# Layer 0's weight preparation: butterflies of the gate and up weights on GpSimd, the down weights' scales applied earlier

## The chip, the cores and the metric

The kernel runs on one core of one Trainium2 chip. The metric is the time of one execution on the device in microseconds (us), and the median over several runs counts. A core has five engines that run their own instruction streams in order: TensorE (PE), which multiplies matrices and writes to PSUM; VectorE (DVE); ScalarE (ACT); GpSimd (POOL); and SyncE (SP), which here only issues DMAs. They wait for each other by semaphores. SBUF is the on-chip memory with 128 partitions, PSUM the accumulation memory.

## The reference: what is computed

The input x has 4 sequences of 512 tokens with 512 features. There are two layers, and each computes

```
xn = layernorm(x)
x  = x + attention(xn) * silu(ffn(xn))
```

Layer 0's attention is a softmax attention with 32 heads of 16 features and 8 key/value heads. Its feed-forward block works in a rotated basis, where `fwht` is the normalised Walsh-Hadamard transform over the last axis:

```
x      = fwht(x * SU_ug) / 64
up     = x @ W_up.T   * (Wscale_ug[:2048] * 64)
gate   = x @ W_gate.T * (Wscale_ug[2048:] * 64)
h      = silu(gate) * up                # 2048 wide
h      = fwht(h * SU_dp) / 64
out    = h @ W_down.T * (Wscale_dp * 64)
```

Layer 1 is a recurrent linear attention with a feed-forward block of signs of weights. The change doesn't touch it.

## The kernel before

The kernel never transforms the tokens. It transforms the weights of layer 0 once, so that the tokens meet plain matrix products. For the gate and up weights a transform of length 512 = 4 x 128 runs over the rows: the 4 blocks are mixed by two butterfly stages (sums and differences of blocks), and the 128 rows within a block by a product with a 128x128 Hadamard matrix that carries the signs `SU_ug` (`hs`). For the down weights it is 2048 = 16 x 128: a product with a matrix `h16`, a trip through memory (`wdt`) that rearranges the rows, and a product with `hmat`; the signs and scales `cdn` (one per row) and `drow` (`Wscale_dp`, one per column) are applied at the last eviction.

The work around the change, with its names:

- `load_raw(n)` (line 166) loads columns of the gate weights (n even) or the up weights (n odd) into a tile `raw` of 128 x 4 x 256 f32. There are n = 0 to 15 such tiles and three buffers.
- `mix(n, stage)` (line 240) calls `butterfly` (line 48) for a stage. Stage 0 reads `raw` and writes `tmp` (one buffer), stage 1 reads `tmp` and writes `raw` back. Each stage is a sum (line 52) and a difference (line 53), each with 128x512 f32 elements on DVE.
- `fold(n, j)` (line 247) multiplies half of `raw` by `hs` on PE (line 253). ACT copies the product as the high part of the weights into `fo` (line 256), DVE subtracts it to get the low part (line 257). After j = 1 the next `load_raw(n + 3)` is issued, and `fo` is stored to memory as `wS` for later sequences.
- `mix_down(q)` (line 268): the first product for the down weights (line 270), a copy out of PSUM by ACT (line 271), a store to `wdt`; after the last q four loads bring it back as `wdn`.
- `fold_down(a)` (line 279): the second product (line 281) into the PSUM tile `y`, of which there is one buffer, and its eviction by DVE with `cdn` and `drow` (line 282).

All this runs while the attention of the first sequence is on its way. The loop over u (line 532) hands out the work by units: per unit one `maxima` (two score products, line 418, and a DVE reduction of 128x1024 from PSUM, line 419, with one buffer of scores), one `exps` eleven units later (line 439 on PE, an exponential on ACT, line 441), one column block of the feed-forward block (from unit 16 on: `gate_up`, line 316, whose PE products are line 326, ACT's tanh line 332, DVE's line 333, ACT's copy line 336 and GpSimd's product `hT` line 337), and from a table `early` the butterflies, folds and first down transforms: `mix(n, 0)` three units and `mix(n, 1)` two units before the two halves of `fold(n)`, at units 12 + 2n and 13 + 2n. `fold_down` has units 32 to 47. Each eight units `values` (line 443) multiplies the exponentials by the values; the sums of the softmax go through memory in four DMA steps (`sum_d`, `rc`, `rec_d`, `sm`), and GpSimd multiplies by their reciprocals (line 465).

The order on an engine is not the order of the program text. A planner orders each engine's instructions by their place in the text and by its own estimate of when their inputs are ready; `inorder` (`keep_in_program_order`) pins single ones. Once planned, each engine takes its instructions strictly in order.

Of the kernel before, what the change touches and what calls it, by code (L numbers as in the profile page):

```python
# [12 lines left out]
AF = mybir.ActivationFunctionType  # L13
ALU = mybir.AluOpType
# [4 lines left out]
P = 128  # L19
NB, SEQ, DM = 4, 512, 512  # L20
NT = NB * SEQ // P
TB = SEQ // P
KC = DM // P
# [10 lines left out]
def kernel(ctx: ExitStack, tc: tile.TileContext, i: dict, out: bass.AP):  # L34
    nc = tc.nc

    def new(pool, shape, dtype, tag, **kw):
        return pool.tile(shape, dtype, tag=tag, name=tag, **kw)
# [6 lines left out]

        return ap.unsqueeze(1).to_broadcast([ap.shape[0], n, ap.shape[1]])

    def butterfly(eng, dst, src, dim, h, pin=lambda ins: ins):

        s = src.rearrange("p (n two h) f -> p n two h f", two=2, h=h)  # L50
        d = dst.rearrange("p (n two h) f -> p n two h f", two=2, h=h)
        pin(eng.tensor_tensor(d[:, :, 0], s[:, :, 0], s[:, :, 1], ALU.add))
        pin(eng.tensor_tensor(d[:, :, 1], s[:, :, 0], s[:, :, 1], ALU.subtract))

    def ln_params(pool, rows, tag):

# [44 lines left out]
    if True:  # L101
# [10 lines left out]
        wdn = new(awp, [P, NI, DM], F32, "wdn")  # L112
# [4 lines left out]
        cdn = new(awp, [P, NI], F32, "cdn")  # L117
        drow = new(awp, [P, DM], F32, "drow")
# [45 lines left out]
        raws, fos = {}, {}  # L164
# [15 lines left out]
        nc.sync.dma_start(su_ug, i["su_ug"])  # L180
        nc.sync.dma_start(wsc, i["wsc"])
        nc.sync.dma_start(su_dp, i["su_dp"])

        stage = [new(hp, [P, DM], F32, "hT", bufs=16) for _ in range(NI)]
        for q in range(NI):
# [23 lines left out]
        for h in (8, 16, 32, 64, 1, 2, 4):  # L209
            nxt = new(a0 if h == 64 else awp, [P, P], F32, "h16" if h == 64 else "hmat", bufs=1 if h == 64 else 2)  # L210
            butterfly(nc.vector, nxt.unsqueeze(2), hmat.unsqueeze(2), P, h, inorder)
            hmat = nxt
            if h == 64:
                h16 = nxt
# [23 lines left out]
        tmps = {}  # L238

        def mix(n, stage):  # L240
            if stage == 0:
                tmps[n] = new(a0, [P, KC, CQ], F32, "tmp")
                butterfly(nc.vector, tmps[n], raws[n], KC, 1)
            else:
                butterfly(nc.vector, raws[n], tmps[n], KC, 2)

        def fold(n, j):
            q, m = n // 2, n % 2
# [19 lines left out]
        def mix_down(q):  # L268
            ph = new(bmm, [P, DM], F32, "mm")
            nc.tensor.matmul(ph, h16, stage[q], start=True, stop=True)  # L270
            nc.scalar.copy(stage[q], ph)
            nc.sync.dma_start(wdt.rearrange("(p q) n -> q p n", q=NI)[q], stage[q])
            if q == NI - 1:
                for o in range(4):
                    nc.sync.dma_start(
                        wdn[:, ts(o, 4), :], wdt[ts(o, DM), :].rearrange("(a p) n -> p a n", p=P)
                    )

        def fold_down(a):
            ph = misc()  # L280
            nc.tensor.matmul(ph, hmat, wdn[:, a, :], start=True, stop=True)
            nc.vector.scalar_tensor_tensor(wdn[:, a, :], ph, cdn[:, a : a + 1], drow, ALU.mult, ALU.mult)

        vps, kTs, oTs, hTs, g0s, wcs, ths = {}, {}, {}, {}, {}, {}, {}

# [71 lines left out]
        def misc(dtype=F32):  # L357

            return new(bpy, [P, SEQ], dtype, "y") if piece[0] % 64 < 32 else new(bmm, [P, SEQ], dtype, "mm")
# [16 lines left out]
        def queries(b, v, jj):  # L376

            pq = misc()
            for k in range(KC):
                nc.tensor.matmul(  # L380
                    pq, wq[:, k, ds(256 * v + P * jj, P)], xnTs[b][:, k, :], start=(k == 0), stop=(k == KC - 1)
                )
            qd = qds[b, v, jj] = new(b0, [P, SEQ], F16, f"qd{jj}", bufs=1)
            nc.scalar.activation(qd, pq, AF.Copy, scale=0.25)
# [122 lines left out]
        keys_values(0)  # L507
        for jj in range(2):
            queries(0, 0, jj)
        nc.sync.dma_start(drow, i["wsc_dp"].to_broadcast([P, DM]))  # L510
        nc.sync.dma_start(wo, i["wo0"].rearrange("(k p) n -> p k n", p=P))

        ph = new(bmm, [P, KC, P], F32, "mm")
# [10 lines left out]
        for n in range(FF // P):  # L524
            u = LATE + 2 * n - 4
            for d, f in ((-3, lambda n=n: mix(n, 0)), (-2, lambda n=n: mix(n, 1)),
                         (0, lambda n=n: fold(n, 0)), (1, lambda n=n: fold(n, 1))):
                early.setdefault(u + d, []).append(f)
        for q in range(NI):
            early.setdefault(q, []).append(lambda q=q: mix_down(q))  # L530

        for u in range(NU + LAG + 1):
# [22 lines left out]
            if 16 <= v < 16 + NI:  # L555
                fold_down(v - 16)
# [297 lines left out]
    total, done, n = sum(x[0] for x in steps), 0.0, 0  # L854
# [17 lines left out]
    drow = new(cm, [P, DM], F32, "drow")  # L872
# [35 lines left out]
    raws = {}  # L908
# [19 lines left out]
    pin, yvs = [False], {}  # L928
# [472 lines left out]
    n = 0  # L1401
# [56 lines left out]
```

## Time and profile before

| What | Value |
|---|---|
| Median of 3 runs | 1495.93 us (1493.04 to 1501.23) |
| Profiled execution, span from first to last instruction | 1492.3 us (no other time is recorded for this execution) |
| PE busy | 1429.4 us (96%), 8144 instructions |
| DVE busy | 1035.8 us (69%) |
| ACT busy | 709.6 us (48%) |
| POOL busy | 313.5 us (21%), 304 instructions |
| Mean granted TensorE clock | 0.992 |
| Line 52 and 53, all butterflies of raw and tmp | 64 instructions, 0.68 us median each, from 15.4 to 152.2 us |
| Line 419, maxima | 256 x 1.22 us |
| Line 257, low part | 32 x 0.68 us |
| Line 282, eviction of the second down transform | 16 x 0.74 us, from 117.7 to 182.8 us |
| Line 271, eviction of the first down transform | 16 x 0.585 us, from 20.2 to 42.1 us |
| Line 337, POOL product hT | 64 x 1.32 us |

A line of the profile's stage view gives a stretch in us from the start of the span, its length, and then for PE, PE's weight loads (PEld), DVE, ACT and POOL the busy time with the number of instructions, then the granted clock, the DMA engines' busy share and GB/s. A line of the timeline gives start, duration, engine, line of the kernel, operation, output<-inputs with shapes, and in brackets the idle time before it with what ended it. Matmuls are pipelined, so that the next begins before the last one's recorded end.

### The profile page before, as it was taken

The numbers are of one execution on the slowest core, as the hardware profiler recorded it, in microseconds if no ns is written. First come the engines' busy times: TensorE is split into PE (matmuls) and PEld (weight loads), VectorE is DVE, ScalarE is ACT, GpSimd is POOL, SyncE is SP. The second block draws the span as 40 slices with busy tenths as digits, with TensorE's granted clock in tenths as the row PEclk, the third lists the DMA queues.
The fourth block names the chain that finished last, engine by engine and source line by source line (L and its number), as shares of the span: only waits on it lengthen the run. The fifth ranks groups of instructions, "written<-read, shape, count | busy, mean of one in ns | idle before, by whom it ended". The sixth has DMA issues, their size and how long they took to land. (4 is left out here: it accounts for less than half of the span.)

```text
span 1492.3 us, 22700 instructions
## 1 busy us (share of the span) xinstructions
PE 1429.4 (96%) x8144; PEld 855.6 (57%) x8144; DVE 1035.8 (69%) x1863; ACT 709.6 (48%) x1046; POOL 313.5 (21%) x304
## 2 busy tenths in 40 slices
PE   7999999999999999999999899999999999999998
PEld 3565533555335553356434576787568766776675
DVE  7999755765557655666525869768975799477746
ACT  4655554666446664466552434434353344323433
POOL 1112100322003220033100330045112531052001
PEclk9999999999999999999999999999999999999989
DMA  8865410475105741166103553434453354425532
GB/s 307 322 220 194 149 29 16 149 237 190 27 21 190 231 149 28 36 212 225 56 20 103 160 146 101 116 92 147 134 151 103 91 161 135 126 73 150 162 83 96
DMA packets 201793, 199.11 MB, mean 133 GB/s; under 512 B 65520, under 2 KB 153040, under 8 KB 200784
## 3 DMA queue, kind: packets, MB, share of 16 engines
q1 hardware_dynamic: 198624, 196.29, 41.9%
q10 hardware_dynamic: 3056, 1.37, 0.4%
q8 instruction: 64, 1.05, 0.3%
q14 instruction: 49, 0.40, 0.1%
HBM read 146.80 MB, written 46.19 MB: 129 GB/s over the span
## 5 line engine op out<-in xcount | busy, mean ns | idle before, releaser
L419 DVE TENSOR_REDUCE nmx<-sc 128x2 f32<-128x1024 f32 x256 | 312.3, 1220 | 159.1 <-PE st L439 147.3
L441 ACT ACTIVATE pe<-st 128x1024 f16<-128x1024 f32 x256 | 262.6, 1026 | 143.4 <-PE st L439 141.6
L344 PE MATMUL y<-wdn,hT 128*128 128x512 f32 x512 | 253.3, 617 | 3.0 <-DVE g L348 1.7
L326 PE MATMUL mm<-xr,wc 128*128 128x512 f32 x768 | 206.8, 410 | 0.0
L326 PEld LDWEIGHTS mm<-xr,wc 128*128 128x128 f32 x768 | 137.4, 189 | 48.4 <-issue 21.8
L337 POOL TENSOR_TENSOR hT<-hT,th 128x512 f32<-128x512 f32 x64 | 84.2, 1316 | 319.2 <-ACT hT L336 309.0
L344 PEld LDWEIGHTS y<-wdn,hT 128*128 128x128 f32 x512 | 87.0, 189 | 96.0 <-issue 88.5
L711 PE MATMUL pu<-xn1T,wp 128*128 128x512 f32 x288 | 129.9, 594 | 0.0
L941 PE MATMUL ph<-xsh,sg 128*128 128x512 f32 x256 | 113.0, 441 | 5.6 <-ACT sg L926 5.3
L418 PE MATMUL sc<-kT,qT 32*128 32x512 f16 x512 | 102.5, 385 | 7.8 <-DVE nmx L419 7.4
L926 ACT ACTIVATE sg<-sw 128x512 fp32r<-128x512 f32 x128 | 79.5, 625 | 55.2 <-PE y L972 32.2
L941 PE MATMUL ph<-xsl,sg 128*128 128x512 f32 x256 | 104.1, 407 | 0.7 <-DVE xsl L901 0.7
L418 PEld LDWEIGHTS <-qT 32*128 32x128 f16 x512 | 26.2, 91 | 131.8 <-issue 127.9
L465 POOL TENSOR_TENSOR oT<-os,sm 128x512 f16<-128x512 f32 x32 | 41.5, 1298 | 285.9 <-DMA sm<-rec_d 248.8
L439 PE MATMUL st<-qm,kT 32*128 32x512 f16 x512 | 100.0, 384 | 0.3 <-ACT pe L441 0.3
L946 ACT ACTIVATE hT<-ph,upsc 128x512 f32<-128x512 f32 x64 | 43.8, 685 | 94.3 <-PE ph L941 94.1
L711 PEld LDWEIGHTS pu<-xn1T,wp 128*128 128x128 f32 x288 | 54.0, 191 | 56.6 <-issue 54.8
L972 PE MATMUL y<-sg,hsh 128*128 128x512 f32 x256 | 83.0, 432 | 0.7 <-ACT sg L926 0.7
L1019 POOL TENSOR_TENSOR gm<-g,le 128x384 fp32r<-128x384 f32 x64 | 57.8, 921 | 83.0 <-PE pu L1020 52.0
L326 PE MATMUL mm<-xr,fo 128*128 128x512 f32 x256 | 73.2, 420 | 0.9 <-DVE fo L257 0.9
L972 PE MATMUL y<-sg,hsl 128*128 128x512 f32 x256 | 73.5, 400 | 0.0
L332 ACT ACTIVATE th<-mm,hwg 128x512 f32<-128x512 f32 x64 | 44.0, 688 | 56.0 <-PE mm L326 56.0
(302 smaller groups left out, 2370.2 us busy)
## 6 DMA issues: line engine op xcount, KB each, us to landing
wc<-wS SPq DMA_DIRECT2D x96, 512.0 KB
wS<-fo SPq DMA_DIRECT2D x16, 1024.0 KB
sw<-in_upT SPq DMA_DIRECT2D x64, 256.0 KB
sw<-in_downT SPq DMA_DIRECT2D x64, 256.0 KB
sm<-rec_d SPq DMA_DIRECT2D x128, 64.0 KB
raw<-in_w_gateT SPq DMA_DIRECT2D x8, 512.0 KB
hT<-in_w_downT SPq DMA_DIRECT2D x16, 256.0 KB
raw<-in_w_upT SPq DMA_DIRECT2D x8, 512.0 KB
```

The source lines that it names most:

```text
L326: nc.tensor.matmul(pgs[m], wcs[b, c, m][:, h, k, :], xrs[b][:, k, :], start=(k + h == 0), stop=(k == KC - 1 and h == 1))
L337: nc.gpsimd.tensor_tensor(hT, hT, ths[b, c], ALU.mult)
L344: nc.tensor.matmul(ys[t], hTs[b, c][:, ts(t, P)], wdn[:, c, :], start=(c == 0), stop=(c == NI - 1))
L418: nc.tensor.matmul(sc[:, j, :], qTs[n][rows, ts(t, P)], kTs[b, g // 4][rows, :], start=True, stop=True)
L419: nc.vector.tensor_reduce(nmxs[n][:, t, 2 * pr : 2 * pr + 2], sc, AX.X, ALU.max, negate=True)
L439: nc.tensor.matmul(st[:, j, :], kTs[b, g // 4][rows, ts(k, P)], qms[n][rows, :], start=True, stop=True)
L441: nc.scalar.activation(pes[u], st, AF.Exp)
L711: nc.tensor.matmul(pp, wps[b, n][:, k, 0:P], xn1Ts[b][:, k, :], start=(k == 0), stop=(k == KC - 1))
L926: tc.keep_in_program_order(nc.scalar.activation(sgs[b, c, m], raws[b, c, m], AF.Sign))
L941: ins = nc.tensor.matmul(ph, sgs[b, c, 0][:, ts(k, P)], xss[b][n][:, k, :], start=(k + n == 0), stop=(k == KC - 1 and n == 1))
L972: ins = nc.tensor.matmul(yss[b][t], hss[b, c][n][:, ts(t, P)], sgs[b, c, 1], start=(c + n == 0), stop=(c == NI - 1 and n == 1))
L1019: nc.gpsimd.tensor_tensor(gm, bc_in(s["g2"][:, t, u, x], P), bc_mid(le, 3), ALU.mult)
```

## The change

`butterfly` may put its differences on another engine than its sums. The butterflies of `raw` go to GpSimd, except the difference of the second stage for n = 3 to 15, which stays on VectorE: one operation in four. The row `drow` is loaded ahead of the weights instead of after the first queries; VectorE multiplies the first down transform by it while it leaves PSUM, in place of ScalarE's copy; and ScalarE instead of VectorE takes the second transform out of PSUM, with the scale `cdn` alone.

```diff
-    def butterfly(eng, dst, src, dim, h, pin=lambda ins: ins):
+    def butterfly(sums, dst, src, dim, h, pin=lambda ins: ins, differences=None):
...
-        pin(eng.tensor_tensor(d[:, :, 0], s[:, :, 0], s[:, :, 1], ALU.add))
-        pin(eng.tensor_tensor(d[:, :, 1], s[:, :, 0], s[:, :, 1], ALU.subtract))
+        pin(sums.tensor_tensor(d[:, :, 0], s[:, :, 0], s[:, :, 1], ALU.add))
+        pin((differences or sums).tensor_tensor(d[:, :, 1], s[:, :, 0], s[:, :, 1], ALU.subtract))
...
         nc.sync.dma_start(su_dp, i["su_dp"])
+        nc.sync.dma_start(drow, i["wsc_dp"].to_broadcast([P, DM]))
...
                 tmps[n] = new(a0, [P, KC, CQ], F32, "tmp")
-                butterfly(nc.vector, tmps[n], raws[n], KC, 1)
+                butterfly(nc.gpsimd, tmps[n], raws[n], KC, 1)
             else:
-                butterfly(nc.vector, raws[n], tmps[n], KC, 2)
+                butterfly(nc.gpsimd, raws[n], tmps[n], KC, 2, differences=nc.vector if n > 2 else nc.gpsimd)
...
             nc.tensor.matmul(ph, h16, stage[q], start=True, stop=True)
-            nc.scalar.copy(stage[q], ph)
+            nc.vector.tensor_tensor(stage[q], ph, drow, ALU.mult)
...
             nc.tensor.matmul(ph, hmat, wdn[:, a, :], start=True, stop=True)
-            nc.vector.scalar_tensor_tensor(wdn[:, a, :], ph, cdn[:, a : a + 1], drow, ALU.mult, ALU.mult)
+            nc.scalar.activation(wdn[:, a, :], ph, AF.Copy, scale=cdn[:, a : a + 1])
...
             queries(0, 0, jj)
-        nc.sync.dma_start(drow, i["wsc_dp"].to_broadcast([P, DM]))
         nc.sync.dma_start(wo, i["wo0"].rearrange("(k p) n -> p k n", p=P))
```

## The prediction

> **What bounds the kernel now.** I read the page's slices first. The change touches only layer 0's preparation of weights, which the listing puts between about 15 and 185 us, so its slices are those at the left edge (37.3 us each).
>
> ```profile
> PE   7999999999999999999999899999999999999998
> DVE  7999755765557655666525869768975799477746
> POOL 1112100322003220033100330045112531052001
> PEclk9999999999999999999999999999999999999989
> ```
>
> VectorE (DVE) is at 90% or more only in slices 2 to 4, GpSimd (POOL) is nearly empty there, and TensorE (PE) reads 9 almost everywhere. So two engines stand at their limit together in this stretch, and the question is which of them sets the pace. The busy time by stage sharpens this (stretch, then us busy of each engine):
>
> ```profile
> 19.50:44.50 25.00, 24.43 (x85) 11.00 (x84) 21.42 (x34) 14.55 (x24) 0.00 (x0) 1.00 0.88 314
> 45.00:80.00 35.00, 33.20 (x162) 18.40 (x162) 33.12 (x43) 21.28 (x30) 3.94 (x3) 1.00 0.80 302
> 80.00:110.00 30.00, 28.58 (x150) 18.59 (x149) 29.54 (x42) 17.02 (x26) 7.28 (x5) 1.00 0.65 224
> 110.00:140.00 30.00, 29.08 (x142) 18.06 (x142) 29.97 (x42) 15.13 (x23) 7.43 (x5) 1.00 0.57 203
> 140.00:170.00 30.00, 27.72 (x136) 17.32 (x135) 26.46 (x44) 17.01 (x23) 5.12 (x4) 1.00 0.41 159
> 200.00:250.00 50.00, 49.51 (x217) 17.21 (x215) 27.97 (x33) 23.37 (x27) 3.81 (x3) 1.00 0.11 28
> ```
>
> Third column PE, fifth DVE, sixth ScalarE (ACT), seventh POOL. From 45 to 170 us DVE is busy 119.1 of 125 us and PE 118.6, so PE is idle for 6.4 us. From 200 to 250 us, with DVE at 56%, PE idles 0.49 of 50 us: that is a PE that nobody holds up. Who holds it up between 45 and 170 us, by the view of waits (us in total, times, longest):
>
> ```profile
> PE sc L418 <- DVE nmx L419: 2.7, 5, 1.1
> PE y L428 <- DVE nm L425: 1.5, 1, 1.5
> PE mm L253 <- DVE fo L257: 1.5, 2, 1.1
> PE mm L326 <- DVE fo L257: 0.9, 2, 0.5
> PE y L281 <- DVE wdn L282: 0.4, 1, 0.4
> PE st L439 <- ACT pe L441: 0.3, 1, 0.3
> ```
>
> All but 0.3 of 7.3 us are waits for DVE (the idle of the windows comes to 6.4; the two views don't cut alike). Thus DVE is the first limit, but PE stands close behind it.
>
> **How close PE is.** The end of a matmul is modelled, so 6.4 us of idle may be too little. I count PE's records from 45 to 170 us and take each at the distance between starts in unbroken rows of the timeline: L326 230 x 0.235 = 54.1; L253 108 x 0.216 = 23.3; L418, 35 pairs x 0.32 = 11.2; L439, 33 pairs x 0.32 = 10.6; L281 24 x 0.43 = 10.3; L449, 16 groups of four x 0.216 = 3.5; L380 8 x 0.216 = 1.7; L428 16 x 0.056 = 0.9. The sum is 115.6, so 9.4 us at most can be won here however fast DVE becomes. 40 us of DVE work may leave, and still less than 10 us come back.
>
> **The change, part by part.**
>
> *Butterflies.* 64 DVE operations of 128x512 f32 (L52, L53, 0.68 us each, 0.60 from start to start) become 51 on POOL (four each for n = 0 to 2, three each for n = 3 to 15) and 13 on DVE. POOL's price has a row of the same shape: L337, 1.27 us alone. So 51 x 1.27 = 65 us go on POOL. From 45 to 170 us POOL has 19.2 (L337) + 4.6 (L465) and gets 39 x 1.27 = 49.5: 73 of 125 us. It does not become full. DVE loses there 41.6 us (L52 and L53, with their stretched ones) and keeps 13 x 0.68 = 8.8.
>
> The stretched ones matter. The timeline (start, us, engine, line):
>
> ```profile
> 53.60 1.27 POOL L337 TENSOR_TENSOR hT<-hT,th 128x512 f32<-128x512 f32 x1 [46.87 <-ACT hT L336]
> 53.70 1.72 DVE L53 TENSOR_TENSOR tmp<-raw 128x512 f32<-128x512 f32 x1
> 81.62 0.68 DVE L257 TENSOR_TENSOR fo<-mm,fo 128x512 fp32r<-128x512 f32 x1
> 81.81 1.27 POOL L337 TENSOR_TENSOR hT<-hT,th 128x512 f32<-128x512 f32 x1 [8.35 <-ACT hT L336]
> ```
>
> A DVE butterfly that begins beside a POOL operation takes 1.72 us instead of 0.68: it stands until POOL is done (53.60 + 1.27), and runs then. L257, with one input in PSUM, is not touched (0.68 beside POOL), and so are the maxima L419 (1.21 beside it). Each of the 13 differences reads the tmp that POOL has just written, and POOL's own sum of the same stage is ready at the same moment; I charge all 13 with 1.72 - 0.68 = 1.04, that is 13.5 us of DVE (between 0 and 13 x 1.27 = 16.5).
>
> The chain of one n hardly grows. Before, from the first L52 of tmp to the last L53 of raw it lasts 4.1 to 9.5 us (n = 5 to 15), since the pieces lie between other DVE work. After, 3 x 1.27 + 0.60 = 4.4, with one L337 between 5.7. Between the end of the chain and its first fold L253 there were 1.4 to 7.1 us for n = 6 to 15. So the fold is not late by this alone: 0.
>
> The Trainium skill, page "GPSIMD Engine Reference", section "4.1 Engine selection", speaks against this: two-input elementwise work belongs on VectorE, since GpSimd is about twice as slow. The rows agree on the ratio (1.27 against 0.68); by the page's own figure (4497 ns at 2048 elements, a quarter of it 1.12 us) the 51 would take an estimated 57 us. By that rule the change loses 51 x 0.59 = 30 us of engine time; by the stage's rows POOL had that time free.
>
> *Second leaves (L282) to ACT.* 16 x 0.74 us leave DVE, 12 of them (8.8 us) before 170 us. On ACT the nearest rows are L271 (copy of the same size, 0.585) and L946 (scale by a column, 0.685): 16 x 0.59 to 0.69 = 9.4 to 11.0. ACT is busy 70.4 of 125 us, which covers it. But behind it in ACT's queue stand the exponentials (1.03), and ahead of it as well, and y, the PSUM tile that L281 writes, has one buffer, so L281 can wait up to 16 x 1.03 = 16 us; below, it gains the 0.4 us above. I take +0.5.
>
> *First transform's eviction (L271) to DVE.* 16 x 0.585 leave ACT; 16 x 0.68 come to DVE (row of the same operands: L958, hT from PSUM and drow, 0.681), all from 20 to 43 us. DVE there: 21.42 of 25, minus ten butterflies x 0.60, plus 16 x 0.60 = 25.0 of 25. So DVE becomes full in this stretch, PE having 0.57 us idle. Bounds: 0 and 9.6 (nothing covered); I take +1, since the sum only just fills it.
>
> *The load of drow* moves ahead of raw and w_down on SP. It is one issue of 0.54 us and 256 KB, 0.8 us at the 314 GB/s above. Behind it wait raw 0 and the stages. Chain 0 ended at 21.3 us and its fold began at 33.1 us: with 0.8 us and the 2.5 us by which 5.1 exceed 2.6 it is still covered, 0. Without that cover 0.8.
>
> **The sum.** With a free DVE, PE keeps about 1% idle (0.49 of 50), so of 6.4 idle 5.1 go, of 9.4 about 8. I take 7.5, near the upper end because half of the DVE load goes: 119.1 - 41.6 - 8.8 + 8.8 + 13.5 = 91 of 125. Against it +1 and +0.5. Net -6.0. The profiled execution's span was 1492.3, the median of the runs is 3.6 above it (the lowest 0.7); I carry the difference unchanged: 1495.9 - 6.0 = 1489.9, that is -0.4%. A measurement of this kernel can tell about 0.5% (7.5 us) from no change.
>
> **The rivals.**
>
> *More is won (0.25).* All 9.4 us go, and PE also gains in 170 to 200 us (0.84 idle) and at the first maxima, which stood behind butterflies until 19.5 us though their scores came at 18.8: up to 12. For it: DVE's waits hold PE in every window. Against it: the bubbles between kinds of matmul stay. 1484 to 1488.
>
> *It gets slower (0.22).* POOL takes its instructions in order, and the butterflies now share its queue with L465, which waits for a chain of DMAs:
>
> ```profile
> 144.54 1.28 POOL L465 TENSOR_TENSOR oT<-os,sm 128x512 f16<-128x512 f32 x1 [4.91 <-DMA wS<-fo]
> ```
>
> Nobody stood behind it then. Now chain, fold and the next load of raw (three buffers) would, and DVE at its next difference with the maxima behind it. With four L465 in the stage at 4.9 us each and 13 differences that hold DVE 2.6 us (a sum and an L337 of POOL), PE's cover of 1.4 to 7.1 us per fold is used up at some: 4 x 4.9 + 13 x 1.0 = 33 at the worst, less the 8 won. It decides once a chain ends later than its fold is due, some 5 us. I price it at +10, 1506. Against it: two of the first three L465 waited 1.3 us or less.
>
> *Nothing shows (0.15).* The order on each engine is made by a planner, and another order may cost as much as DVE gives: PE stays at 118.6 of 125. 1494 to 1498. That POOL does not get the work cannot be, the engine is named.
>
> The forecast has 0.38. Its own range is 1487 to 1492, its gain beyond 7.5 us in about a third. So faster by over 0.5%: 0.12 + 0.24 = 0.36; slower by over 0.5%: 0.18; within: 0.46. The range reaches into the first two rivals: 1482 to 1505.
>
> **What would show it.** Right: DVE near 70 to 75% from 45 to 165 us, POOL near 60%, waits of PE for L419 and L257 nearly gone, the last L257 (ended 166.7 us) some 6 us earlier, everything after it shifted and else unchanged. The first transforms' end (L270, last began 41.1 us) shows the +1. Wrong: idle time of POOL put down to a DMA before L465, DVE waiting for POOL's tmp, PE L253 waiting for raw, or L281 waiting for ACT. The forecast fails most easily by the planner's order.

## The result and the profile after

The changed kernel takes 1503.63 us (median of 20 runs, 1496.86 to 1511.64), the kernel before 1495.84 us in runs beside it (20 runs). The ratio is 1.0048, 95% interval 1.0033 to 1.0063: slower by 0.5%, 7.2 us, where I had forecast 6.0 us less. The profiled execution of the changed kernel has a span of 1497.8 us (before 1492.3) at a granted clock of 0.993. From line 183 to line 509 the listing of the changed kernel is one line further down: L257 before is L258 after, and so on; `hk` (L516) and all behind it keep their numbers.

The page's slices after, the same rows as shown of before (40 slices of 37.4 us):

```profile
PE   6999999999999999999999899999999999999998
DVE  8966545766557655576524869768975799467746
POOL 5367200323003220033100240046112531052001
PEclk9999999999999999999999999999999999999989
```

VectorE has fallen in slices 3 and 4 (from 99 to 66) and GpSimd has risen there. What should have followed, a fuller PE, isn't seen. By stage (columns as before: length, PE, PEld, DVE, ACT, POOL, granted clock, DMA share, GB/s):

```profile
19.50:44.50 25.00, 21.89 (x71) 8.00 (x70) 24.76 (x34) 4.55 (x6) 11.01 (x9) 1.00 0.71 253
45.00:80.00 35.00, 32.88 (x161) 19.33 (x162) 30.14 (x45) 22.21 (x30) 17.56 (x14) 1.00 0.95 348
80.00:110.00 30.00, 27.32 (x139) 17.64 (x137) 20.76 (x27) 16.34 (x25) 20.66 (x17) 0.94 0.55 189
110.00:140.00 30.00, 28.87 (x142) 18.41 (x142) 19.05 (x24) 17.56 (x27) 23.34 (x18) 1.00 0.63 231
140.00:170.00 30.00, 29.08 (x140) 17.79 (x139) 17.38 (x24) 18.99 (x29) 11.29 (x9) 1.00 0.36 137
```

From 45 to 170 us DVE is busy 87.3 us (119.1 before), POOL 72.9 (23.8), and PE 118.2 (118.6): 32 us of DVE went and PE got none of it. From 19.5 to 44.5 us PE is idle 3.1 us where it was 0.57. What PE waits for from 45 to 170 us (total, times, longest):

```profile
PE y L429 <- DVE nm L426: 3.9, 4, 2.0
PE sc L419 <- DVE nmx L420: 1.7, 2, 1.5
PE mm L327 <- DVE fo L258: 0.7, 2, 0.6
```

The waits for the low parts (L257 before) and for the maxima have shrunk as forecast, from 2.4 and 2.7 us to 0.7 and 1.7. In their place stands L426, the second of two tiny DVE operations (128x16) that turn the maxima into a matmul operand: 3.9 us instead of 1.5.

The deficit can be followed by PE's work: the busy time of PE up to a given moment, matmuls at half clock counted as half. Against before, it is -1.2 us at 25, -2.8 at 40, -2.3 at 80, -6.4 at 90, -4.1 at 170, and layer 1's first product (L760) begins at 796.1 us instead of 791.6. So two places lose: 20 to 40 us, and 80 to 90 us.

**The first place.** VectorE's timeline there (start, us, engine, line); it has the four `hk` (signs times Hadamard, an input of the matrix `hs`) and the row scales `cdn`, all tiny and all in SBUF:

```profile
18.52 0.84 DVE L516 TENSOR_SCALAR hk<-hmat,su_ug 128x128 f32<-128x128 f32 x1 [0.51 <-PE mm L517]
21.01 0.92 DVE L516 TENSOR_SCALAR hk<-hmat,su_ug 128x128 f32<-128x128 f32 x1
23.25 1.24 DVE L233 TENSOR_TENSOR cdn<-wsc 128x16 f32<-128x16 f32 x1
25.02 0.70 DVE L234 TENSOR_TENSOR cdn<-cdn,su_dp 128x16 f32<-128x16 f32 x1
26.24 0.82 DVE L235 TENSOR_SCALAR cdn<-cdn 128x16 f32<-128x16 f32 x1
```

In the timeline of before, the same operations have their own length:

```profile
19.29 0.28 DVE L516 TENSOR_SCALAR hk<-hmat,su_ug 128x128 f32<-128x128 f32 x1
22.91 0.17 DVE L232 TENSOR_TENSOR cdn<-wsc 128x16 f32<-128x16 f32 x1
```

A 0.17 us operation lasts up to 1.24 us. From 15.4 to 30.8 us GpSimd does the twelve butterflies of n = 0 to 2 without a break, 1.27 us each. These are two of them:

```profile
23.15 1.31 POOL L52 TENSOR_TENSOR raw<-tmp 128x512 f32<-128x512 f32 x1
24.42 1.26 POOL L53 TENSOR_TENSOR raw<-tmp 128x512 f32<-128x512 f32 x1
```

The first `cdn` operation ends at 24.49 (23.25 + 1.24), when the first of these is done (24.46); the second ends at 25.72, when the other is (25.68). So a small operation on VectorE stands here until the butterfly under way is done. Five of the eight such operations are held, for 3.5 us in all, on an engine that was to be full anyway; the other three, begun within 0.3 us of the end of a butterfly, lasted 0.16 to 0.29 us. What PE waits for from 19.5 to 44.5 us (the two longest lines; the kernel before has none in this stretch):

```profile
PE mm L271 <- DVE hT L272: 1.1, 3, 0.7
PE mm L517 <- DVE hk L516: 0.8, 1, 0.8
```

The longest wait for an eviction, 0.7 us, ended with the L272 that began at 24.42, behind the held `cdn`. In these same 25 us the first fold begins at 37.2 us instead of 33.1, the last first transform (L270) at 48.4 instead of 41.1, and the load into the first raw buffer that comes free is issued at 42.7 instead of 36.5. That the held operations are the reason for all of this is so far argued; the experiments below test it.

**The second place.** The timeline around 85 us, on three engines:

```profile
84.28 1.27 POOL L53 TENSOR_TENSOR tmp<-raw 128x512 f32<-128x512 f32 x1
84.76 0.84 DVE L425 CAST nm<-nmx 128x16 f16<-128x16 f32 x1
85.50 1.26 POOL L338 TENSOR_TENSOR hT<-hT,th 128x512 f32<-128x512 f32 x1
85.64 1.21 DVE L426 TENSOR_TENSOR nm<-nmx,nm 128x16 f16<-128x16 f32 x1
86.91 0.61 PE L429 MATMUL y<-ident,nm 128*128 128x128 f16 x4 [2.01 <-DVE nm L426]
```

Cast and subtraction (about 0.2 us each when alone) are held by one butterfly and one product of GpSimd, PE stands for 2.0 us, and the next 3.4 us are granted at half clock. A stall of 2.0 us thus became one of 3.7.

### The profile page after: what moved, and what is told of

It reads as the page before. It is cut to its first block, busy times and chain, and to the rows that moved or that the text cites. A ratio compares the mean times of both kernels' runs of the same rounds, so it can differ in the third digit from the quotient of the medians.

```text
span 1497.8 us, 22727 instructions
## 1 busy us (share of the span) xinstructions
PE 1430.7 (96%) x8144; PEld 854.7 (57%) x8144; DVE 1006.6 (67%) x1812; ACT 709.0 (47%) x1046; POOL 379.7 (25%) x355
## 4 chain that ended last, share of the span: by engine, by line
PE 65%; DVE 19%; DMA 7%; issue 4%; ACT 2%; POOL 2%; SPq 1%; DVEq 0%; ACTq 0%; POOLq 0%
PE y L345 16%; PE mm L327 13%; PE ph L941 5%; PE sc L419 4%; PE y L972 4%; PE pu L711 3%; DVE nmx L420 2%; DVE yc L719 2%; PE mm L450 2%; DVE UT L1075 2%; PE pu L1032 1%; DVE sx L1071 1%; PE pu L1208 1%; PE pu L760 1%; PE pu L1269 1%
## 5 line engine op out<-in xcount | busy, mean ns | idle before, releaser
L466 POOL TENSOR_TENSOR oT<-os,sm 128x512 f16<-128x512 f32 x32 | 40.8, 1275 | 284.6 <-DMA sm<-rec_d 258.9
```

## The experiments

All ratios are to the kernel before, in runs beside each on the same chip, with 95% intervals. 0.001 is 1.5 us.

**The parts by themselves.** First the butterflies alone (e1), without the row and both evictions:

```diff
-                butterfly(nc.vector, tmps[n], raws[n], KC, 1)
+                butterfly(nc.gpsimd, tmps[n], raws[n], KC, 1)
...
-                butterfly(nc.vector, raws[n], tmps[n], KC, 2)
+                butterfly(nc.gpsimd, raws[n], tmps[n], KC, 2, differences=nc.vector if n > 2 else nc.gpsimd)
```

> Butterflies as in the change, both evictions and the load of drow as before. Theory A (the +7 us come from VectorE taking the first transform's evictions while it is full, and the butterflies are neutral): 0 to -4 us against before. Theory B (the butterflies on GpSimd hold VectorE's operations with SBUF inputs, in the first 30 us its small ones, later the maxima's casts, and this is the loss): +3 to +7 us.

Measured: 1498.65 us, 1.0051 (1.0030 to 1.0072). Then the rest of the change alone, with the butterflies on VectorE (e2):

```diff
+        nc.sync.dma_start(drow, i["wsc_dp"].to_broadcast([P, DM]))
...
-            nc.scalar.copy(stage[q], ph)
+            nc.vector.tensor_tensor(stage[q], ph, drow, ALU.mult)
...
-            nc.vector.scalar_tensor_tensor(wdn[:, a, :], ph, cdn[:, a : a + 1], drow, ALU.mult, ALU.mult)
+            nc.scalar.activation(wdn[:, a, :], ph, AF.Copy, scale=cdn[:, a : a + 1])
```

> Butterflies on VectorE as before, drow, both evictions as in the change. VectorE then has 25.0 + 3.6 us of work for the 25 us from 19.5 to 44.5. Theory A: +4 to +8 us. Theory B: within 2 us of before, since nothing new stands on GpSimd.

Measured: 1503.85 us, 1.0083 (1.0056 to 1.0109). (VectorE's load in the expectation is too small: the ten butterflies that stay are 6.0 us by the prediction's figures, not 3.6.) Each part by itself costs as much as both together or more, so the parts don't add: with butterflies on VectorE the evictions disturb more than with butterflies on GpSimd. That shows when the first transform alone is put back on ScalarE in the changed kernel (e3; the row is then left out):

```diff
-            nc.vector.tensor_tensor(stage[q], ph, drow, ALU.mult)
+            nc.scalar.copy(stage[q], ph)
```

> The changed kernel, but ScalarE copies the first transform out of PSUM as before; the row of the down weights' scales is left out altogether, so that VectorE loses 16 x 0.68 us and nothing replaces it. Theory A: 4 us or more faster than the change, that is 0 to +3 us against before. Theory B: as the change, +5 to +8 us.

Measured: 1496.87 us, 1.0033 (1.0017 to 1.0050). Within the change the first eviction costs some 2 us (1.0048 against 1.0033, intervals overlap). Splitting e2 further, with butterflies on VectorE: the row at the first transform and VectorE taking the second with the column only (e7); and ScalarE taking the second, the row left out (e8).

```diff
-            nc.scalar.copy(stage[q], ph)
+            nc.vector.tensor_tensor(stage[q], ph, drow, ALU.mult)
...
-            nc.vector.scalar_tensor_tensor(wdn[:, a, :], ph, cdn[:, a : a + 1], drow, ALU.mult, ALU.mult)
+            nc.vector.tensor_scalar(wdn[:, a, :], ph, cdn[:, a : a + 1], None, ALU.mult)
```

> Butterflies on VectorE as before; VectorE applies the row at the first transform, and it also takes the second out of PSUM, with the column alone. So VectorE gets 16 x 0.6 us from 20 to 45 us, and nothing leaves it. If the loss of the evictions (about +7 us at equal clock) is the load on VectorE from 20 to 45 us: +6 to +9 us. If it is ScalarE at the second transform: +1 to +3 us.

Measured: 1502.72 us, 1.0071 (1.0051 to 1.0091).

```diff
-            nc.vector.scalar_tensor_tensor(wdn[:, a, :], ph, cdn[:, a : a + 1], drow, ALU.mult, ALU.mult)
+            nc.scalar.activation(wdn[:, a, :], ph, AF.Copy, scale=cdn[:, a : a + 1])
```

> Butterflies on VectorE and the first transform's copy on ScalarE as before; the second transform leaves PSUM by ScalarE with the column alone, and the row of scales is left out. If VectorE's load from 20 to 45 us is the loss of the evictions: 0 to -2 us (12 x 0.66 us less on a full VectorE from 117 us on). If ScalarE at the second transform is the loss: +4 to +6 us.

Measured: 1494.12 us, 1.0007 (0.9991 to 1.0024): no cost of the second leaves can be told. The cost of e2 stays with the first eviction. (e2 and e7 also load the row early; but so does e3, which is not slower than e1.) The trace of e7 shows by what means: the order on VectorE puts butterflies behind evictions. The butterflies of n = 0, 1, 2 are done at 36.7, 46.1 and 56.9 us (before 21.3, 26.8, 30.6), and the folds of n = 1 and 2 begin at 49.7 and 57.6 instead of 37.6 and 42.3. The stage lines of e7 (columns as above) show the price and the clock that goes with it:

```profile
19.50:44.50 25.00, 21.75 (x69) 7.83 (x68) 24.26 (x37) 4.84 (x6) 0.00 (x0) 0.91 0.71 241
45.00:80.00 35.00, 32.66 (x144) 17.91 (x143) 32.37 (x46) 17.58 (x24) 2.76 (x2) 0.92 0.78 286
```

**How much there was to win, and where GpSimd's presence takes it.** The kernel before with all butterflies left out (e4; the folds then read raw weights), and the same with 51 operations on GpSimd that read raw and write tmp, which nobody reads (e6).

```diff
-                butterfly(nc.vector, tmps[n], raws[n], KC, 1)
+                pass
...
-                butterfly(nc.vector, raws[n], tmps[n], KC, 2)
+                pass
```

> The kernel before without any butterfly of raw and tmp: the folds take raw as loaded. It shows what VectorE's load of 64 x 0.60 us costs at most. The prediction's theory (TensorE waits 6.4 to 9.4 us for VectorE from 45 to 170 us): -6 to -10 us. Theory C (TensorE's waits are those of a chain and of the planned order, VectorE's load has little part in them): -3 us or less.

Measured: 1485.89 us, 0.9962 (0.9944 to 0.9980): 5.7 us (3.0 to 8.4 by the interval) are all that a VectorE without butterflies brings.

```diff
-                butterfly(nc.vector, tmps[n], raws[n], KC, 1)
+                butterfly(nc.gpsimd, tmps[n], raws[n], KC, 1)
...
-                butterfly(nc.vector, raws[n], tmps[n], KC, 2)
+                nc.gpsimd.tensor_tensor(d[:, :, 0], s[:, :, 0], s[:, :, 1], ALU.add)
+                if n < 3:
+                    nc.gpsimd.tensor_tensor(d[:, :, 1], s[:, :, 0], s[:, :, 1], ALU.subtract)
```

> No butterfly counts (the folds take raw as loaded), but GpSimd does the change's 51 operations on the same tiles, raw to tmp, and nobody reads tmp. Against the kernel without butterflies (5 to 6 us faster than before) this shows what their presence costs without anyone waiting for their data. Theory of the shared access (operations of GpSimd hold VectorE's): +3 us or more against the kernel without butterflies, of them most before 40 us. Theory of the chain (folds and VectorE's differences wait for GpSimd's results): within 1.5 us of it.

Measured: 1493.85 us, 1.0000 (0.9982 to 1.0017). The unread operations cost what leaving the butterflies out had won, though nothing reads their results (one reload of `raw` waited for them, 0.3 us). So a loss of about this size (5.7 us, with an uncertainty of some 3.7) arises by GpSimd's activity without late chains or differences that wait. The trace of e6 shows a way from the held operations to PE:

```profile
24.39 1.25 DVE L231 TENSOR_SCALAR hwg<-wsc 128x16 f32<-128x16 f32 x1
25.76 1.23 DVE L233 TENSOR_TENSOR cdn<-cdn,su_dp 128x16 f32<-128x16 f32 x1
27.02 1.19 DVE L234 TENSOR_SCALAR cdn<-cdn 128x16 f32<-128x16 f32 x1
28.12 1.21 DVE L423 TENSOR_REDUCE nmx<-sc 128x2 f32<-128x1024 f32 x1
29.39 0.39 PE L422 MATMUL sc<-kT,qT 32*128 32x512 f16 x2 [1.81 <-DVE nmx L423]
```

Three scale operations, 0.17 us each in the kernel before, keep VectorE until 28.1 us, the maxima stand behind them, and PE waits 1.8 us for the maxima. Is it the early stretch? The butterflies of n = 0 to 2 go back to VectorE, the rest as in e1 (e5):

```diff
-                butterfly(nc.gpsimd, tmps[n], raws[n], KC, 1)
+                butterfly(nc.gpsimd if n > 2 else nc.vector, tmps[n], raws[n], KC, 1)
...
-                butterfly(nc.gpsimd, raws[n], tmps[n], KC, 2, differences=nc.vector if n > 2 else nc.gpsimd)
+                butterfly(nc.gpsimd if n > 2 else nc.vector, raws[n], tmps[n], KC, 2, differences=nc.vector)
```

> The butterflies alone (as in the first experiment), but those of n = 0 to 2 stay on VectorE; both evictions as before. If the first experiment's loss of about 5 us arises where GpSimd works on the first three tiles (15 to 31 us) and holds VectorE's small operations on hk and cdn: 0 to +1 us against before. If it arises later, in the stretch from 45 to 170 us: +4 to +6 us as in the first experiment.

Measured: 1506.29 us, 1.0092 (1.0071 to 1.0113), a miss by its time. Its trace says two things: PE's work is back to that of before (within 0.1 us of it at 25, 40 and 44 us; e1 is 4.9 short at 40), so the early loss is gone; and then stalls of 2.7 and 2.9 us bring half clock for 6.8 us from 48.0 and 3.4 us from 153.8. A new order of the later work hides the answer. So the small operations are moved instead, and the butterflies left in place: `hk` to ScalarE, the four scale operations (the first is shown) to GpSimd.

```diff
-            inorder(nc.vector.tensor_scalar(hwg, wsc[:, 0, :], 0.5 / DM**0.5, None, ALU.mult))
+            inorder(nc.gpsimd.tensor_scalar(hwg, wsc[:, 0, :], 0.5 / DM**0.5, None, ALU.mult))
...
-            inorder(nc.vector.tensor_scalar(hk, hmat, su_ug[:, k : k + 1], None, ALU.mult))
+            inorder(nc.scalar.activation(hk, hmat, AF.Copy, scale=su_ug[:, k : k + 1]))
```

This edit was made in the changed kernel (e9), in the butterflies alone (e11), and in the kernel with unread operations (e13).

> The changed kernel with VectorE's small early operations taken out of GpSimd's reach: ScalarE makes hk, GpSimd itself the four scale operations. In the changed kernel GpSimd's butterflies stretch these from 0.17 to 0.29 us each to 0.7 to 1.24 us, 3.5 us in all, between 17 and 27 us. Theory of the shared access: 2 to 4 us faster than the change (+3 to +5 us against before). If the early loss is VectorE's evictions alone: within 1 us of the change (+7 us).

Measured: 1496.93 us, 1.0013 (0.9992 to 1.0034).

> The butterflies alone (evictions as before), with hk on ScalarE and the scale operations on GpSimd. Theory of the shared access: the early loss of the first experiment (3 us by 40 us, and a stretch of half clock at 30 us) goes: 3 to 5 us faster than that, 0 to +2 us against before. If not: +5 to +6 us as there.

Measured: 1496.48 us, 1.0024 (1.0009 to 1.0039).

> As the run with unread operations on GpSimd (no butterfly counts, the folds take raw as loaded), with hk on ScalarE and the scale operations on GpSimd. If holding these early operations was the cost of GpSimd's presence (5.7 us between that run and the kernel without butterflies): 3 to 5 us faster than before. If it was the later operations of the maxima: 0 to -1 us against before.

Measured: 1487.23 us, 0.9953 (0.9938 to 0.9969). The edit brings 5.2, 4.0 and 7.0 us, each with an uncertainty of 3.5 to 3.9. Between e1 and e11, where the evictions are those of before, the first fold moves from 39.1 to 35.2 us and the last first transform from 48.3 to 43.7, and PE's work at 40 us, 4.9 us short in e1 (1.7 of it by half clock from 29.8 us), is 1.3 short in e11. Between the changed kernel and e9 the traces show less, 2.8 short and 1.8 short at 40 us. In e13 all that GpSimd's activity had cost is back. The stage from 19.5 to 44.5 us of e6, and then that of e13:

```profile
19.50:44.50 25.00, 22.47 (x75) 9.30 (x75) 19.39 (x22) 12.29 (x20) 10.93 (x9) 1.00 0.77 260
```

```profile
19.50:44.50 25.00, 24.23 (x83) 9.97 (x83) 16.34 (x21) 15.42 (x28) 11.83 (x11) 1.00 0.82 282
```

PE gains 1.8 us in 25, with no less GpSimd work beside it (11.8 us for 10.9). In e6 DVE isn't full in this stage (19.4 of 25), so it wasn't short of time; PE waited for single operations that stood. One control is missing: the same edit in the kernel before. Its eight operations last 1.8 us in all there (4 x 0.28 + 4 x 0.17), so the edit may bring up to that much without any GpSimd. But PE of the kernel before idles for 0.57 us in this stage, and the view of waits has no wait of PE from 17 to 45 us there, so little of the gain can come from these 25 us. That the edit also helps by another planned order is not excluded.

**The maxima's cast.** Cast on ScalarE and the low part of the maxima left out, in the changed kernel (e10) and, as control, in the kernel before (e12):

```diff
-            nc.vector.tensor_copy(nmg[:, :, :, 0], nmxs[n])
-            nc.vector.tensor_tensor(nmg[:, :, :, 1], nmxs[n], nmg[:, :, :, 0], ALU.subtract)
+            nc.scalar.copy(nmg[:, :, :, 0], nmxs[n])
```

> The changed kernel, but the maxima are rounded by ScalarE and their low part is left out (it stays zero), so VectorE has no operation with SBUF inputs between the maxima and TensorE's transposes. In the changed kernel TensorE waits 3.9 us for these, once for 2.0 us with a stretch of half clock behind it. Theory of the shared access: 3 to 6 us faster than the change. If the planned order decides: within 2 us of it.

Measured: 1486.09 us, 0.9948 (0.9937 to 0.9960).

> Control for the second kernel of this call: the kernel before with the maxima's cast on ScalarE and the low part left out. Both theories: 0 to -3 us against before, since TensorE waited 1.5 us once for it there and GpSimd seldom works beside it.

Measured: 1480.96 us, 0.9920 (0.9900 to 0.9940). The control gets 12 us faster by the edit, the changed kernel 15. Without the control, e10 would have passed for proof that the second place is the cause. The difference, 3 us with an uncertainty of some 4, isn't told from nothing; it fits the 3.5 us that PE's work loses from 85 to 90 us. Why the edit brings 12 us in the kernel before stays open. Only the cast moved, with the low part kept, in the kernel before (e15) and in e11 (e16):

```diff
-            nc.vector.tensor_copy(nmg[:, :, :, 0], nmxs[n])
+            nc.scalar.copy(nmg[:, :, :, 0], nmxs[n])
```

> The kernel before with the maxima's cast alone on ScalarE, the low part kept on VectorE: nothing of the computation is left out. Leaving out the low part too gave -12 us. If what counts there is VectorE's operation with SBUF inputs and its place in the queue: -2 to -6 us. If it is the length of the chain from the maxima to the transposes (an engine more in it): 0 to +5 us.

Measured, in the kernel before: 1492.48 us, 0.9988 (0.9972 to 1.0005).

> The butterflies alone with the small early operations and the maxima's cast moved, nothing left out: a candidate to beat the kernel before. If the cast helps as its removal did: -2 to -6 us against before; if not, as without it: +2 to +4 us.

Measured, in e11: 1495.33 us, 1.0013 (0.9997 to 1.0030). Neither is told from no change.

**The differences that stay on VectorE.** e11 with every butterfly on GpSimd (e14):

```diff
-                butterfly(nc.gpsimd, raws[n], tmps[n], KC, 2, differences=nc.vector if n > 2 else nc.gpsimd)
+                butterfly(nc.gpsimd, raws[n], tmps[n], KC, 2)
```

> The butterflies alone with the small early operations moved, and the last quarter of the butterflies (13 differences) on GpSimd as well, so that VectorE never stands in its queue for GpSimd's tmp (12.6 us in seven waits in the run it starts from). If these waits are what uses up the gain from 45 to 170 us: 2 to 5 us faster than that run, -1 to -3 us against before. If GpSimd's chain to the fold is the limit: 1 to 4 us slower than that run, since each chain grows by 0.7 us.

Measured: 1494.29 us, 1.0006 (0.9987 to 1.0025): 2.7 us below e11, with intervals that overlap. It leaves nothing out and still isn't faster than before, while e13, with the same work on VectorE, 13 operations fewer on GpSimd and no one reading their results, is 7 us faster than before. The trace of e14 has a second place again, at 145 us:

```profile
145.43 0.89 DVE L424 CAST nm<-nmx 128x16 f16<-128x16 f32 x1
146.35 1.21 DVE L425 TENSOR_TENSOR nm<-nmx,nm 128x16 f16<-128x16 f32 x1
147.62 0.40 PE L428 MATMUL y<-ident,nm 128*128 128x128 f16 x4 [2.02 <-DVE nm L425]
```

In e13 the same step falls between two GpSimd operations, and costs PE little:

```profile
143.56 0.19 DVE L428 CAST nm<-nmx 128x16 f16<-128x16 f32 x1
143.79 0.23 DVE L429 TENSOR_TENSOR nm<-nmx,nm 128x16 f16<-128x16 f32 x1
144.07 0.40 PE L432 MATMUL y<-ident,nm 128*128 128x128 f16 x4 [0.36 <-DVE nm L429]
```

Whether this is where e14's missing gain lies was tried last: e14 with the edit of e10 (e17), and e14 with only the cast moved (e18).

> All butterflies on GpSimd, the two groups of small VectorE operations moved off, and the maxima's cast on ScalarE with its low part left out. Theory A, the relief of VectorE is lost again at the maxima's cast and subtraction: the time falls by more than the control lost by the same edit (12 us), to 1475 to 1478 us beside 1494. Theory B, the cast costs the kernel before as much: 1481 to 1484 us, and what is missing lies in the planned order.

Measured: 1482.54 us, 0.9934 (0.9912 to 0.9957).

> The same with the low part kept, so that nothing is left out: only the cast moves to ScalarE, the subtraction stays on VectorE. Theory A: 3 to 5 us below the version with the cast on VectorE, 1489 to 1492 us. Theory B: as the control, 1 to 2 us, 1492 to 1494 us.

Measured: 1495.01 us, 1.0018 (1.0002 to 1.0035). e14 gets 11 us faster by the edit (1.0006 to 0.9934), within the noise as much as the control, and not faster by the smaller one. So nothing shows that the maxima's step keeps e14 from being faster; theory A falls. What remains, some 7 us between e13 and e14, comes with real dependence on the butterflies and 13 more of them on GpSimd. The order the planner makes of it may carry it, which isn't shown; which instruction does stays open. No version that leaves nothing out beat the kernel before.

## Why the prediction was wrong

- **What bounds the kernel, and its size.** The view was right: VectorE's waits hold PE, and little is to be had. (VectorE is at 90% or more in slices 25, 29, 33 and 34 too, outside the stretch.) With no butterflies at all 5.7 us are won (e4) where I took 7.5 with 13 of them and their stretching left. By the middle of e4's interval that was too much by some 2 us.
- **DVE and POOL load.** Right: DVE 70% from 45 to 170 us (forecast 70 to 75), POOL 58% (60), GpSimd not full, waits of PE for the maxima and low parts shrunk. But the last low part ended at 171.1 us, 4.4 later than before instead of some 6 earlier.
- **The step that failed** is the one on the stretched operations. I saw that a DVE operation beside a GpSimd one stands until that is done, and applied it to the operations that the change moves (the 13 differences), and declared the two biggest of the others untouched, which they are. I didn't go through VectorE's remaining operations for those that are small, read only SBUF, and lie where GpSimd would now work without a break: `hk`, the scales, the maxima's cast. Moving `hk` and the scales away turns the change from 1.0048 to 1.0013 (e9), 5.2 us with an uncertainty of some 3.9, of which at most 1.8 may be due to the removed work itself. The fault is one of the sum: under "Butterflies" it priced the operations that move and their own chain ("So the fold is not late by this alone: 0") and had no term for what they do to their neighbours. The Trainium skill, page "SBUF — State Buffer", section "Who interferes with whom", says that a VectorE operation with two SBUF inputs, a cast or a tensor_scalar may contend with GpSimd for a shared port pair, that whoever holds it blocks the other for the whole instruction, and that a reduction doesn't contend. The rows agree: `cdn` 0.17 to 1.24, the cast 0.2 to 0.84 and once 1.32, the maxima's reduction (out of PSUM) 1.16 to 1.23 throughout.
- **The relief, -7.5, also failed in its own stage.** Against before, PE's work from 45 to 170 us (one execution each) grew by 4.5 us in e4 and 4.3 in e13, where no fold waits for a butterfly. In the changed kernel it fell by 2.1: 3.5 were lost between 85 and 90 us at the second place, and only 1.4 gained elsewhere; in the other runs whose folds read GpSimd's butterflies and which leave nothing out it lay between -3.3 (e16) and +1.7 (e18), in e5 at -9.1. PE didn't wait for `raw` in the changed kernel (the view has no such line), so it isn't the sign that the prediction named; what takes the relief there stays open.
- **13 differences at 1.04 us stretched (13.5 us of DVE).** The sum was near, the form was not: they lasted 0.687 us on average, and VectorE instead stood idle before them. The view of waits, VectorE, 20 to 200 us:

```profile
DVE raw L53 <- POOL tmp L53: 12.1, 6, 2.7
```

  By e14 against e11 it cost 2.7 us of time, with intervals that overlap, so it isn't told from nothing.
- **First transform's eviction, +1.** About 2 us within the change (e3), and 10 to 12 alone (e2, e7). DVE was full from 19.5 to 44.5 us, as worked out (24.8 of 25 busy); but +1 took a full engine as the only harm, where the order on it matters: the last L270 began 7 us later, not 1.
- **Second leaves, +0.5.** Right within what can be measured: e8 1.0007, and on ScalarE 0.689 us each where 0.59 to 0.69 was forecast.
- **The load of drow, 0.** No run shows it by itself; e3, which has it and the second leaves beside the butterflies, is not slower than e1 (1.0033 against 1.0051). In the changed kernel the first load of `raw` is issued 0.5 us later (5.3 instead of 4.8), the next two 1.6 us later, and the first butterfly begins at 15.4 us as before.
- **The rivals.** The sign was that of "it gets slower", but not its mechanism: GpSimd had no idle time before its four L466 of the stretch. It stood before butterflies instead, for the load of `raw` (16.2 us in two waits), and PE had no wait for it. A part of its second half was true, DVE standing at its next difference.

Put together: forecast -6.0; the relief smaller by 1.8, the small operations +5.2, the first eviction +1, make +2. Measured +7.2. The rest of 5 us has candidates that the runs don't settle: the maxima's step (3 us, e10 against e12) with the half clock after the stall at 85 us (1.7 us of it in the profiled execution; the mean granted clock over the 20 runs is 0.9907, over 125 runs of the kernel before beside the experiments 0.9918), the differences (2.7 us, e14 against e11), and the planned order, the way of failing that the prediction's last line names. Neither the 3 nor the 2.7 us is told from nothing by the runs, and the 5.2 of the small operations is itself uncertain by 3.9.

## What to carry to other kernels

Before giving GpSimd long elementwise work, list what VectorE has left in that stretch, not only what moves: each small SBUF-only operation on it (a cast, a column scale, a tile of 16 columns) can be held for a whole GpSimd operation, and on a path to PE the wait counts, however little busy time it is. Run every experiment that leaves work out in the kernel before as well: here the most convincing one (15 us won) won 12 us without the change. And where each engine's order is planned, a part moved alone may cost more than with the others, so price parts inside the change.

## What the runs showed of the hardware

- **Half clock after a slack slice.** The granted clock falls in steps of 3.41 us, on a fixed grid within an execution. I cut the profiles of all 20 kernels here on that grid and looked at what followed each slice at full clock. After slices with PE busy under 45%, the next was at half clock in 47 of 49 cases; between 45 and 75% in 51 of 305; at 75% or more in none of some 8,100. In the changed kernel the slice from 83.4 to 86.8 us holds 1.9 us of the one wait of 2.0, and PE is busy for 1.49 of 3.4 us (44%); these lines are that slice and the one after it (columns as above):

```profile
83.40:86.80 3.40, 1.49 (x8) 0.71 (x6) 3.37 (x6) 0.59 (x1) 3.40 (x4) 1.00 0.31 58
86.80:90.20 3.40, 3.29 (x11) 1.96 (x11) 2.07 (x4) 1.08 (x2) 2.39 (x2) 0.50 0.97 360
```

  The Trainium skill, page "TensorE: Matmul & The Clock Gate", section "HAM oscillation — how this bites in real kernels", asks for no idle gaps of PE above about 3.4 us. Here a gap of 2.0 us was enough, and the measurement decides: a stall of 1.9 us within one slice can nearly double its own price, by 1.7 us (half of 3.41).
- **A tiny operation can cost as much as a big one.** 128x16 elements on VectorE took 0.17 us (`cdn` in the kernel before) to 1.32 us (a cast at 116.8 us in the changed kernel), by whether GpSimd was at a 128x512 f32 operation (1.27 us).
- **GpSimd is held too.** Its sums of the second stage (L52, raw from tmp) took 1.50 us on average where those of the first stage took 1.28. Seven of the sixteen took 1.77 to 1.80 us, and each of these began 0.04 to 0.05 us after VectorE's difference of the same stage; with all butterflies on GpSimd (e14) none took over 1.31.
